# Where a transformer kernel forms its softmax totals and small weight sums: a change of places

## The chip, the cores and the metric

The kernel runs on one core of a Trainium2 chip. The core has a matrix engine (TensorE, written PE; its weight loads PEld), a vector engine (DVE), an activation engine (ACT), a general engine (GpSimd, written POOL) and SyncE (SP), whose queue (SPq) here only issues DMAs. The metric is the device time of one execution in microseconds. Three executions before the change took 2140.83, 2141.53 and 2144.35 us; the median is 2141.53.

## What is computed

The program runs two transformer layers over 16 sequences ("jobs" b = 0 to 15) of 256 tokens with 256 features, all in float32. Each layer has self attention, cross attention to a context and a feed-forward part:

```
x = attn(adaln(x), adaln(x)) @ wo + bo + x          # self, 16 heads of 64 in layer 0
x = attn(adaln(x), ln(context)) @ wo + bo + x       # cross
x = gelu(adaln(x) @ w1 + b1) @ w2 + b2 + x          # feed-forward
# layer 1 is the same with 16 heads of 16 and other modulations
```

The attention is softmax(q k^T / sqrt(d)) v, with rotary positions in layer 0. The softmax is taken without subtracting a maximum. Its denominators ("totals") are formed beside the products and multiplied into the attention's result before the output product.

## The kernel before

**Phases, jobs, steps.** Six phases follow each other: layer 0 self, layer 0 cross, layer 0 feed-forward, and the same three of layer 1. In each phase the jobs run b = 0 to 15; an attention job has two steps (s = 0, 1), a feed-forward job four. One list of steps is walked in order, and each engine's instructions stand in the order in which this walk writes them (a manual schedule). So an engine never passes over an instruction that waits, and the DMAs of SP are issued in the order written.

**One attention step of layer 0** (two groups of four heads, u = 2s and 2s + 1) does, for the current job, the rest of softmax and attention, and at the same time the preparation of the next step ("then"):

- The scores of the step were multiplied at the end of the step before (`scores`, `stage_s`, L768, on PE; L781, the exponentials, on ACT).
- `stage_t` (L787), `stage_turn` (L793) and `stage_reduce` (L800), all on DVE, add the exponentials over the two halves of the keys, transpose in blocks of 32 and sum. After four of each, job["rows"] is complete.
- `layer0_sums` (PE L839, ACT L849) multiplies the exponentials with the values; the result is job["raw"], four parts.
- For the next step, queries and keys are multiplied (`keys`, `query_part`, by Strassen's seven products once b is large enough: `queries_by_seven`, from b = 3 in self and from b = 4 in cross attention; `stage_rotary` with eight products before that). `rotate` and `stage_rotary` multiply by cosine and sine on DVE (L629, L636, L725) and form sums on POOL (L643, L733). The next scores need all of these sums.

**Totals.** `sum_up(job, at)` multiplies the rows with a small matrix on PE (`form_total`, "fold,rows"), takes the reciprocal on DVE (L813), sends it to DRAM by SP (L816) and fetches it back spread over the partitions (L819, which waits for the first DMA to land). `scale(job, *which)` multiplies parts 0 to 3 with it on POOL (L828). `fold_inner` then forms sums of the parts on POOL (L1121) for the output product, which `finish_folded` does in the next step in seven products, numbered 1 to 7, on PE; its additions to x follow on DVE (L1137 to L1148). `finish` (L1168) is the same with the plain product.

Where a job's total is formed depends on the step that follows it. From cross 4 on, `finish_folded(late, ..., total=job)` forms the current job's total at the end of its second step, so that the scaling in the next step ("early") finds it ready. Before that, and in self attention, the total of the previous job ("late") is formed in the first step of the next job, by sum_up(late, ...), and used in that same step.

**Weights' sums.** Strassen's products need sums of weights. `fold_query_weights` (POOL, L558 to L561) forms four of them for each half of the query weights; in cross attention the second half follows at the end of step s = 1 of b = 3, and query_part needs it from the next step on. `fold_output_weights` (DVE, L1031 to L1034) forms four for the feed-forward's second weight: in layer 0 in job 1's third step, in layer 1 in job 2's first, just after `pair_hidden` (L990, L1010, L1011, L1017, L1018 on DVE). `output_products(done, ...)` then does products 1 and 2 of the job two before in a second step, the others (4, 5, 6, 7, 3) in its fourth.

**The border.** `leaving` is true for b = 15 of a layer 0 attention phase. Its first step also loads the first half of the next phase's weights ("first") on SP, at the top of the step and so ahead of the step's totals. In cross attention, the job before it (14) gets its output product by finish(late, 7) in the second step of job 15, since no attention of layer 0 follows.

**Start.** `idle_products(n)` is n products of the identity with itself, into a bank that nothing reads. One call of 2 stands before `prepare_input(jobs[0])`.

## Time and profile before

| | |
|---|---|
| median of three runs | 2141.53 us |
| profiled execution | 2143.74 us |
| its span, first to last instruction | 2141.9 us |
| granted PE clock, mean over the span | 0.998 |
| ACT busy, DVE busy, POOL busy | 931.5, 1697.6, 1375.6 us |
| scores' products of a step in layer 0 (L768, x128) | 3.64 us |
| one scaling on POOL (L828), median | 1.28 us |
| one sum of parts on POOL (L1121), two tensors | 1.62 us mean |

The page has one row for each engine (busy time, share of the span, instructions). The chain of waits follows the last instruction back, at each point to what released it. The list of waits gives, for each pair of waiter and releaser, the sum, the number and the longest. The timeline gives the start and the length of instructions, equal neighbours merged with their number, and in brackets the idle time of the engine before it with what ended it. A PE product here is recorded as several matmul instructions that run side by side, so that the spacing of their starts, not their length, says how fast PE goes.

Where layer 0's self attention ends, the steps of PE stand so: self 14/1 from 603.04, self 15/0 from 623.09, self 15/1 from 642.21, cross 0/0 from 663.90 us (each after its scores).

### The profile page before, as it was taken

The numbers are of one execution on the slowest core, as the hardware profiler recorded it, in microseconds if no ns is written. First come the engines' busy times: TensorE is split into PE (matmuls) and PEld (weight loads), VectorE is DVE, ScalarE is ACT, GpSimd is POOL, SyncE is SP. The second block draws the span as 40 slices with busy tenths as digits, with TensorE's granted clock in tenths as the row PEclk, the third lists the DMA queues.
The fourth block names the chain that finished last, engine by engine and source line by source line (L and its number), as shares of the span: only waits on it lengthen the run. The fifth ranks groups of instructions, "written<-read, shape, count | busy, mean of one in ns | idle before, by whom it ended". The sixth has DMA issues, their size and how long they took to land.

```text
span 2141.9 us, 115148 instructions
## 1 busy us (share of the span) xinstructions
PE 2125.1 (99%) x52400; PEld 1472.1 (69%) x52400; DVE 1697.6 (79%) x3108; ACT 931.5 (43%) x1527; POOL 1375.6 (64%) x1498
## 2 busy tenths in 40 slices
PE   9999999999999999999999999999999999999998
PEld 5666767767766667677676768886665565566887
DVE  5878888888888888999998867865777777777765
ACT  3334334334333333443443344433666666665442
POOL 4888778778768788787878756662322223235773
PEclk9999999999999999999999999999999999999999
DMA  6110110110132321212212033221212232223321
GB/s 197 28 41 24 27 40 23 29 38 23 36 102 71 80 56 36 68 36 54 50 48 53 23 77 92 56 50 22 63 40 43 49 99 63 58 48 85 73 64 39
DMA packets 307050, 118.00 MB, mean 55 GB/s; under 512 B 243364, under 2 KB 289784, under 8 KB 306424
## 3 DMA queue, kind: packets, MB, share of 16 engines
q1 hardware_dynamic: 305320, 108.71, 20.6%
q8 instruction: 412, 6.75, 1.4%
q10 hardware_dynamic: 1232, 1.84, 0.2%
q14 instruction: 86, 0.70, 0.1%
HBM read 77.14 MB, written 33.29 MB: 52 GB/s over the span
## 4 chain that ended last, share of the span: by engine, by line
PE 85%; POOL 3%; DVE 3%; issue 1%; DMA 1%; SPq 0%; ACT 0%; DVEq 0%; POOLq 0%; ACTq 0%
PE banks L84 54%; PE banks L768 15%; PE banks L839 9%; PE banks L858 5%; PE banks L704 1%; PE banks L503 1%; POOL raw L828 1%; POOL folded L1121 1%; POOL qk L733 0%; DMA spread<-sums_seen 0%; DMA sums_seen<-inv 0%; DVE x L1075 0%; DVE m L629 0%; POOL qk L643 0%; DVE xh L365 0%
## 5 line engine op out<-in xcount | busy, mean ns | idle before, releaser
L781 ACT ACTIVATE pr<-banks 128x1024 f32<-128x1024 f32 x576 | 487.3, 937 | 450.1 <-PE banks L768 413.8
L643 POOL TENSOR_TENSOR qk<-m,m 128x256 f32<-128x256 f32 x400 | 303.9, 788 | 78.8 <-DVE m L636 47.2
L839 PE MATMUL banks<-pr,v 128*32 128x256 f32 x4096 | 244.8, 379 | 0.0
L768 PE MATMUL banks<-qk 32*64 32x256 f32 x8192 | 242.0, 379 | 2.6 <-POOL qk L643 1.8
L787 DVE TENSOR_TENSOR both<-pr 128x1024 f32<-128x1024 f32 x128 | 182.8, 1428 | 63.2 <-ACT pr L781 59.8
L768 PEld LDWEIGHTS banks<-qk 32*64 32x64 f32 x8192 | 186.2, 132 | 62.4 <-POOL qk L643 21.1
L828 POOL TENSOR_TENSOR raw<-raw,spread 128x512 f32<-128x512 f32 x128 | 168.5, 1337 | 50.8 <-DMA spread<-sums_seen 40.3
L839 PEld LDWEIGHTS banks<-pr,v 128*32 128x32 f32 x4096 | 131.4, 110 | 85.0 <-issue 16.8
L453 POOL TENSOR_TENSOR x<-x,bo_b 128x256 f32<-128x256 f32 x96 | 73.2, 782 | 163.2 <-DVE xh L365 163.2
L900 POOL TENSOR_TENSOR oT<-oT,spread 128x256 f32<-128x256 f32 x64 | 45.8, 738 | 205.3 <-DVE spread L899 205.3
L849 ACT COPY raw<-banks 128x512 f32<-128x512 f32 x128 | 75.0, 587 | 197.6 <-PE banks L839 192.5
L793 DVE STREAM_TRANSPOSE squares<-both 128x1024 f32<-128x1024 f32 x128 | 158.1, 1235 | 2.2
L800 DVE TENSOR_REDUCE rows<-squares 128x32 f32<-128x1024 f32 x128 | 154.8, 1209 | 0.9
L629 DVE TENSOR_TENSOR m<-banks,rope 128x512 f32<-128x512 f32 x200 | 128.3, 683 | 21.7 <-PE banks L84 12.1
L1121 POOL TENSOR_TENSOR folded<-raw,raw 128x512 f32<-128x512 f32 x90 | 143.5, 1623 | 2.4
L858 PE MATMUL banks<-pr,wide_v 128*32 128x256 f32 x2048 | 134.3, 379 | 0.0
L768 PE MATMUL banks<-q,k 32*64 32x256 f32 x4096 | 127.9, 381 | 0.0
L636 DVE TENSOR_TENSOR m<-banks,rope 128x512 f32<-128x512 f32 x200 | 125.2, 676 | 1.7 <-POOL qk L643 0.8
L84 PE MATMUL banks<-hT,wk_sa 128*32 128x256 f32 x2048 | 126.2, 381 | 0.0
L1075 DVE TENSOR_TENSOR x<-banks,x 128x256 f32<-128x256 f32 (+2 forms) x150 | 79.6, 531 | 56.1 <-PE banks L84 49.8
L768 PEld LDWEIGHTS banks<-q,k 32*64 32x64 f32 x4096 | 87.5, 131 | 37.7 <-issue 13.6
L733 POOL TENSOR_TENSOR qk<-m,m 128x512 f32<-128x512 f32 x56 | 78.3, 1419 | 35.3 <-DVE m L725 32.4
(289 smaller groups left out, 4577.8 us busy)
## 6 DMA issues: line engine op xcount, KB each, us to landing
turned<-blocks SPq DMA_DIRECT2D x380, 64.0 KB
fetched<-turned SPq DMA_DIRECT2D x380, 64.0 KB
spread<-sums_seen SPq DMA_DIRECT2D x128, 128.0 KB
x<-in_x SPq DMA_DIRECT2D x16, 256.0 KB
fetched_c<-turned_c SPq DMA_DIRECT2D x64, 64.0 KB
cT<-in_ctx_turned SPq DMA_DIRECT2D x16, 256.0 KB
out<-x SPq DMA_DIRECT2D x15, 256.0 KB
ctx<-in_ctx SPq DMA_DIRECT2D x16, 192.0 KB
```

Of the source, the lines that this page charges most:

```text
L84: nc.tensor.matmul(out[cut], lhsT[:, cut], rhs, start=start, stop=stop, **more)
L629: nc.vector.tensor_tensor(view, bank(2 + e if job["cross"] else 2 * e).rearrange("p (t h n) -> p t h n", t=2, h=2), rope[:, i, :].rearrang ...
L643: nc.gpsimd.tensor_tensor(out, cos[i], sin[1 - i], (ALU.subtract, ALU.add)[i])
L768: nc.tensor.matmul(banks[64 * g : 64 * g + 64, at + h, t * N : (t + 1) * N], lhs, rhs, start=(half == 0 and (t == 0 or job["layer"] == 1)) ...
L781: nc.scalar.activation(pr[:, one], sc[:, one], AF.Exp, scale=0.125 if job["layer"] == 0 else 0.25)
L787: nc.vector.tensor_tensor(both, pr[:, :, 0, :], pr[:, :, 1, :], ALU.add)
L793: nc.vector.transpose(job["squares"].rearrange("p b k -> p (b k)"), job.pop("both").rearrange("p h n -> p (h n)"))
L800: nc.vector.tensor_reduce(job["rows"][:, u, :], job.pop("squares"), AX.X, ALU.add)
L828: nc.gpsimd.tensor_tensor(part, part, spread[:, u : u + 1, :].to_broadcast([P, 2, N]), ALU.mult)
L839: nc.tensor.matmul(o[32 * h : 32 * h + 32, half, :], v[:, t, col : col + 32], pr[:, h, t, :], start=(t == 0), stop=(t == NT - 1),)
L858: nc.tensor.matmul(o[32 * h : 32 * h + 32], v[:, t, 4 * c + h, 32 * e : 32 * e + 32], pr[:, h, t, :], start=(t == 0), stop=(t == NT - 1),)
L1121: eng.tensor_tensor(folded[m], *sums[m])
```

## The change

All of it is in where instructions are written; none of the operations changes.

- Every step that is followed by a step of cross attention now passes total=job to finish_folded, so totals are formed at the second step's end for self 15 and cross 0 to 3 as well. `early` is computed for all branches, and in the branch without seven products the scaling is cut in two: parts 0 and 1 after the first rotary pair, 2 and 3 where all four were.
- In self 15/0, sum_up(late) goes up to just behind the first keys, into bank 3; scale(late, 0, 1) goes between rotate(1, 1) and rotate(0, 0), and 2 and 3 stay at the end.
- In cross 15/0 (`leaving`), parts 1, 2 and 3 are scaled together, and the output product of cross 14 is done here, ahead of the scores; finish(late, 7) in 15/1 is gone.
- fold_query_weights for the second half goes from the end of cross 3/1 to its beginning.
- fold_output_weights in layer 1 goes from job 2's first step to its second, behind output_products(done, 1, 2); the weights that are no sums (1 and 2) are set without it.
- The call of idle_products before the first input has 1 in place of 2.

```diff
@@ fold_output_weights, output_products
+        ph.setdefault("output_w", {1: b[0][0], 2: b[1][0]})
...
-        ph["output_w"] = {1: b[0][0], 2: b[1][0], 3: b[1][1], 4: t4, 5: t1, 6: t2, 7: t3}
+        ph["output_w"].update({3: b[1][1], 4: t4, 5: t1, 6: t2, 7: t3})
...
+        weights = job["phase"]["w"]["wo"]
+        job["phase"].setdefault("output_w", {1: weights[:, 0:4, 0:P], 2: weights[:, 4:8, 0:P]})
@@ before the loop
-    idle_products(2)
+    idle_products(1)
@@ feed-forward, s == 0
-            if b == 2 and s == 0:
-                if layer0:
-                    add()
-                else:
-                    fold_output_weights(job["phase"], nc.vector)
+            if b == 2 and s == 0 and layer0:
+                add()
@@ feed-forward, s == 1
                     output_products(done, 1, 2)
+                if b == 2 and not layer0:
+                    fold_output_weights(job["phase"], nc.vector)
@@ attention of layer 0, ahead of the branches
+            if weights_after == 1 and job["cross"]:
+                fold_query_weights(job["phase"], weights_after, nc.gpsimd)
+                weights_after = None
+            early = s == 0 and late is not None and "spread" in late
@@ cross, seven products
                 rotate(then, 1, 1)
                 if early:
-                    scale(late, 1)
+                    scale(late, *((1, 2, 3) if leaving else (1,)))
...
+                if s == 0 and leaving:
+                    add_late = finish(late, 7, later=True)
                 rotate(then, 0, 0)
                 query_part(then, 6)
                 rotate(then, 1, 0)
+                if s == 0 and leaving:
+                    add_late()
+                elif s == 0:
+                    scale(late, 2, 3)
                 if s == 0:
-                    scale(late, *((2, 3) if early else range(4)))
                     stage_turn(job, 1)
@@ self, seven products
                 keys(then, 0, 0)
-                if seven:
+                if s == 0:
                     sum_up(late, 3)
...
-                elif s == 0:
-                    sum_up(late, 6)
...
                     rotate(then, 1, 1)
+                    if s == 0:
+                        scale(late, 0, 1)
                     layer0_sums(job, 2 * s + 1, 5)
...
                     stage_turn(job, 2 * s + 1)
                     if s == 0:
-                        scale(late)
+                        scale(late, 2, 3)
@@ without seven products
                 rotary(then, 0, 1)
...
-                if late is not None and s == 0:
+                if early:
+                    scale(late, 0, 1)
+                elif late is not None and s == 0:
                     sum_up(late, 6)
@@ end of the step
                 if then and then[0]["cross"]:
-                    finish_folded(late, (4, 5), total=job if queries_by_seven(then) else None)
+                    finish_folded(late, (4, 5), total=job)
...
-                else:
-                    finish(late, 7)
             if late is not None and s == 0:
                 if not queries_by_seven(then):
-                    scale(late)
+                    scale(late, *((2, 3) if early else range(4)))
```

## The prediction

> **What bounds the kernel now.** The page's first part comes first. TensorE (PE) is busy in 99% of the span, and the chain of waits gives it 85%, so only time in which PE waits can be won or lost. The list of waits and the timeline then show where PE really stops: a few places, all at borders between phases. A step is called here by phase, job and step: "self 15/0" is the first step of the sixteenth job of layer 0's self attention.
>
> ```profile
> PE 2125.1 (99%) x52400; PEld 1472.1 (69%) x52400; DVE 1697.6 (79%) x3108; ACT 931.5 (43%) x1527; POOL 1375.6 (64%) x1498
> ...
> POOL raw L828 <- DMA spread<-sums_seen: 40.3, 18, 4.6
> ```
>
> The first line is the page's, the second one of the waits: 40.3 us in which the scaling on GpSimd (POOL) sat at the head of its queue until the spread sums had landed. Today hardly anything that PE needs soon is queued behind it.
>
> **Self 15/0: the scaling is put ahead of the rotary sums.** This is the timeline of that step (start, length, engine).
>
> ```profile
> 627.71 0.34 DVE L813 RECIPROCAL inv<-banks 128x32 f32<-128x32 f32 x1
> ...
> 628.75 0.56 SPq L283 DMA_DIRECT2D wk_ca<-in_ca_wkv  x1
> 629.40 1.40 SPq L284 DMA_DIRECT2D wq_ca<-in_ca_wq  x1
> 630.86 0.46 SPq L436 DMA_DIRECT2D ctx<-in_ctx  x1
> 631.44 0.39 SPq L816 DMA_DIRECT2D sums_seen<-inv  x1
> 633.09 2.81 POOL L643 TENSOR_TENSOR qk<-m,m 128x256 f32<-128x256 f32 x4 [2.68 <-DVE m L636]
> ...
> 636.11 1.42 POOL L643 TENSOR_TENSOR qk<-m,m 128x256 f32<-128x256 f32 x2 [0.20 <-DVE m L629]
> 636.28 1.94 SPq L819 DMA_DIRECT2D spread<-sums_seen  x4
> ...
> 638.57 3.71 PE L768 MATMUL banks<-qk 32*64 32x256 f32 x128
> ...
> 641.19 5.98 POOL L828 TENSOR_TENSOR raw<-raw,spread 128x512 f32<-128x512 f32 x4 [3.65 <-DMA spread<-sums_seen]
> ```
>
> The reader is to see that the sums land at 641.19, 2.6 us after PE has begun the next scores at 638.57. The change forms the total some 2 us earlier (just behind the first keys, 623.1). But the DMA of the reciprocals (L816) is not late for want of them: the reciprocal ended at 628.05, and SP was issuing without a break from 622.48 on (8 transposing DMAs, then two weight loads of 512 KB each and a context load, all ahead of L816 in the program, before and after). So L816 stays at 631.44 and the landing at 641.19. What moves is the scaling of the first two parts: it goes ahead of the last four rotary sums (L643, rotations 0/0 and 1/0), which the scores need. POOL reaches it at 634.5 (two of the four L643 at 633.09 are done), waits to 641.19, scales twice (2.53, from the pair at 595.65 in self 14/0), then forms the pair of L643 for the first scores (1.42): 645.15. PE can do 0.43 of the scores with the first of the two, so its new stall is 645.15 - 0.43 - 638.57 = **6.2 us**. The second pair comes at 646.6 and PE needs it 1.8 us after the first: no more.
>
> [...] L816 was issued at 631.44, and the spread, which waits for it, at 636.28, 4.4 us after SP had become free; one megabyte of weights is ahead in the same queue. In self 14/0, with no weights ahead, the same two issues are 588.53 and 590.75[...]. I take 641.19; the ends are 2.8 and 6.8.
>
> A stall of that length also costs clock. The table by windows, around PE's largest stall of today (cross 15/0; the columns are length, busy time of PE, PEld, DVE, ACT, POOL, then the granted clock and the DMAs):
>
> ```profile
> 1244.20:1247.60 3.40, 1.35 (x30) 0.80 (x38) 3.30 (x6) 0.00 (x0) 2.20 (x4) 1.00 0.64 207
> 1247.64:1251.05 3.41, 3.41 (x77) 2.60 (x69) 3.12 (x7) 1.08 (x2) 3.31 (x5) 0.50 0.09 27
> ```
>
> With PE busy 1.35 of 3.40 us, the next 3.41 us run at half clock, and after a full busy window the clock is back. Half clock lasts to the end of the first mostly busy window after the stall, so, with the phase unknown, 1.3 to 3.0 us are lost; I take **2.1**.
>
> Against this stands what a later PE no longer waits for at the border: in self 15/1 PE stands 0.83 and 0.34 for L1121 (its inner sums, which are late because the scaling came at 641.19) and 0.63 and 0.1 for the additions behind it. PE comes some 8 us later, POOL 2 (its folds end near 653.9 instead of 652.0), so all **1.9** go. Part: 6.2 + 2.1 - 1.9 = **+6.4**.
>
> **Totals early in self 15/1 and cross 0 to 3.** PE wins nothing directly: in cross 0 to 2 it has no stall today. New is that a total is formed in the second step, between products 7 and 6, and that PE waits there if the row sums (L800) are late. In cross 0/1, 1/1 and 2/1 they end at 696.03, 735.81 and 772.96; PE gets there near 697.8, 736.2 and 775.0: no wait, at worst 0.3 in the second. The first two scalings now go between the rotary pairs of the next step: in cross 1/0 POOL's second pair then ends at 718.6 instead of 717.5, and PE needs it at 719.3. SP now waits for the sums before the transposing DMAs of the step's end, as it does from cross 4 on. Cost 0; without that cover 0.5 to 1.
>
> **Query weights' sums at the start of cross 3/1.** Four POOL instructions, 1.70 + 0.73 + 1.71 + 0.74 = 4.9 us from the rows at 819.94 to 825.06. Today they lie behind the step and PE waits for two of them in the next: 0.96 + 0.47 = 1.4. Moved, they stand in POOL's queue ahead of this step's rotary sums, and POOL is late there already:
>
> ```profile
> 806.68 1.43 POOL L643 TENSOR_TENSOR qk<-m,m 128x256 f32<-128x256 f32 x2
> ...
> 812.03 1.29 DVE L629 TENSOR_TENSOR m<-banks,rope 128x512 f32<-128x512 f32 x2 [1.13 <-POOL qk L643]
> 813.24 1.21 DVE L800 TENSOR_REDUCE rows<-squares 128x32 f32<-128x1024 f32 x1
> ...
> 814.50 0.22 PE L84 MATMUL banks<-fold,rows 128*32 128x32 f32 x1 [0.99 <-DVE rows L800]
> ```
>
> Each line waits for the one before: POOL's L643 frees DVE's buffers, DVE's L629 holds up the row sum L800, and PE's total waits for that, 1.2 us today. POOL works from 792.6 to 814.8 without a break. New: two of the four scalings (2.5) move into cross 3/0, where POOL had only 1.5 idle, so they push 1.1; less 2.5, plus 4.9, makes it 1.1 - 2.5 + 4.9 = **3.5** later, and PE's total with it (near 818). PE's stall there becomes 4.7, 4.35 of it in one piece (the seventh product waits first for its own operand). Against it, the 1.4 in cross 4/0 go. Clock: the Trainium skill, "TensorE: Matmul & The Clock Gate", Part 1 ("The HAM clock gate"), lets the clock fall after at least one idle window of some 3.4 us. The 4.35 us hold a whole one in (4.35 - 3.41)/3.41 = 28% of phases, so nothing would be the likely cost. But in the first window row above PE was busy for 1.35, and the clock fell: some 2.5 us idle are enough, and 4.35 leave that in one window in three of four phases. I take the row: 0.77 x 2.1 = 1.6; ends 0 and 3.0. Part: 3.5 - 1.4 + 1.6 = **+3.7**. If POOL had the time free, it would be -1.4 to -2.6.
>
> **The last output product a step sooner (cross 15).** 128 PE instructions, 6.9 us by the 7.0 of the row at 1255.91, go from 15/1 into 15/0's stall, where PE waits 2.0 + 0.6 and then loses 1.7 at half clock. The third scaling ends near 1246.9, the product near 1251.3, the scores near 1255: 4.1 ahead of today. But what ends last is another chain. Row sums of job 15 need DVE for some 8 us behind the scores' exponentials (three kinds, two of each, 1.2 each, starting at about 1255.5): they end near 1263.5, against 1261.1 today, and PE, which now reaches the total at 1260.7, waits 3 us there; today the product covered this time and the total ran at 1264.33. Then the sums go through SP behind the transposing DMAs, as today, and land:
>
> ```profile
> 1275.15 5.01 POOL L828 TENSOR_TENSOR raw<-raw,spread 128x512 f32<-128x512 f32 x4 [4.58 <-DMA spread<-sums_seen]
> ```
>
> PE's product of job 15 follows these four scalings until 1280.2. Half clock after the new wait (one phase in three) would be taken from PE's 0.9 of waiting there. So 4.1 won becomes **-0.2**; ends -4.3 and +1.5.
>
> **Output weights' sums in layer 1's feed-forward 2.** Four DVE instructions, 0.69 each:
>
> ```profile
> 1959.33 1.07 PE L84 MATMUL banks<-inner,w_b 128*32 128x256 f32 x16 [1.38 <-DVE sums L1010]
> ```
>
> This wait (1.56 by the matmuls' spacing) goes. Behind L1011 of the second step the four end near 1960.3, and product 4 of the same job needs the last of them; PE would be there at 1959.5. New wait 0.85. Part **-0.7**; ends -1.6 and +0.5.
>
> **One idle product fewer.** Two PE instructions at half clock, 0.85 us at 9.6 to 11.4; PE's work then starts that much sooner, 0.43 in full-clock work. At 39.69 PE comes just as hT of job 1 is ready (it waited 7.6 for its DMA, behind SP's 13 loads of x up to 27.78), so the gain ends there: **0**; ends -0.4 and +1.7 (the clock rising a window later).
>
> **Sum.** 6.4 + 0 + 3.7 - 0.2 - 0.7 + 0 = **+9.2 us** on the profiled span of 2141.9 (the execution took 2143.74, 1.8 around it, which stay). On the median of 2141.53 that is **2150.7**.
>
> **Rivals.**
> - The sums land in time in self 15/0 (not slower). Each us by which they land after 635.0 (638.57 + 0.43 - 3.95) costs PE one; at or before it the step costs nothing and only the 1.9 are won: -1.9 + 3.7 - 0.9 = +0.9, 2142.4. For it: the total is formed 2 us sooner. Against it: SP's unbroken row of issues. 0.08.
> - The query sums do no harm (POOL makes up the 3.5): 6.4 - 1.4 - 0.9 = +4.1, 2145.6. For it: the scaling leaves POOL's queue there. Against: the unbroken POOL. 0.1.
> - All stalls are filled, -1.9 - 2.6 - 4.3 - 1.6: near 2131. It needs both of the above and a DVE that is sooner done in cross 15. 0.08.
> - Each new stall draws long half clock and 15/1's total another: +14, 2155.5. 0.1.
> - The forecast: 0.64, 2147 to 2155.
>
> About 0.2%, 4.3 us, is what a measurement can tell from no change. Faster is the third rival, 0.09 with small shares of others; same the first and half of the second, 0.13; slower the rest, 0.78. The range 2144 to 2158 leaves out the first and third rival and a little above.
>
> **What would show it.** Right: a PE wait of 5 to 7 us before L768 near 639, released by POOL L643, with POOL L828 waiting for the spread just ahead; half clock after it; no waits for L1121 at the border; the total in cross 3/1 waiting over 4 us for L800; that of cross 15 waiting 2 to 3; product 4 in layer 1's feed-forward waiting for DVE's fourth output-weight sum. Wrong: L816 issued before the weight loads, or POOL idle ahead of cross 3/1.

## The result and the profile after

| | before | after |
|---|---|---|
| median, four runs each | 2141.77 us | 2154.70 us |
| profiled execution | 2143.74 us | 2154.66 us |
| its span | 2141.9 us | 2152.8 us |

The change makes the kernel slower: the ratio is 1.0059, with a 95% interval of 1.0041 to 1.0076. The forecast was 2150.7 us, in a range of 2144 to 2158. By the medians the loss is 12.9 us; the profiled execution of before was 2.0 us above its median, so the two profiles differ by 10.9.

Where these 10.9 us come from can be read off the starts of the scores' products (L768 in the timeline), which both kernels do in the same order:

| PE begins | before | after | later by | gained since the row above |
|---|---|---|---|---|
| scores of self 15/0 | 619.25 | 619.17 | -0.08 | -0.1 |
| scores of self 15/1 | 638.57 | 645.14 | +6.57 | +6.7 |
| scores of cross 0/1 | 679.07 | 686.25 | +7.18 | +0.6 |
| scores of cross 4/1 | 835.38 | 842.66 | +7.28 | +0.1 |
| last scores ahead of cross 15 | 1231.04 | 1239.03 | +8.00 | +0.7 |
| first scores of layer 1 | 1469.75 | 1477.22 | +7.47 | -0.5 |
| last scores of layer 1 | 1930.31 | 1937.41 | +7.11 | -0.4 |
| end of the span | 2141.9 | 2152.8 | +10.96 | +3.9 |

So two places make the loss: the border behind self attention (7.3) and layer 1's feed-forward (3.9). The page's first part, which answers to the one shown of before, does not tell this: PE is busy in 99% of either span.

```profile
PE 2128.1 (99%) x52398; PEld 1472.1 (68%) x52398; DVE 1697.2 (79%) x3108; ACT 931.1 (43%) x1527; POOL 1370.9 (64%) x1498
```

The list of waits does, a little: the scaling's waits for its spread are fewer than before (15 for 18), but one is far longer (7.3 us for 4.6).

```profile
POOL raw L828 <- DMA spread<-sums_seen: 43.5, 15, 7.3
```

**Self 15/0.** The timeline of after, in the form in which that of before was shown:

```profile
625.33 0.34 DVE L813 RECIPROCAL inv<-banks 128x32 f32<-128x32 f32 x1
...
629.76 1.10 SPq L284 DMA_DIRECT2D wq_ca<-in_ca_wq  x1
...
631.49 0.39 SPq L816 DMA_DIRECT2D sums_seen<-inv  x1
...
637.38 1.93 SPq L819 DMA_DIRECT2D spread<-sums_seen  x4
...
641.92 2.48 POOL L828 TENSOR_TENSOR raw<-raw,spread 128x512 f32<-128x512 f32 x2 [7.33 <-DMA spread<-sums_seen]
...
644.36 2.77 POOL L643 TENSOR_TENSOR qk<-m,m 128x256 f32<-128x256 f32 x4
645.14 6.44 PE L768 MATMUL banks<-qk 32*64 32x256 f32 x128 [6.42 <-POOL qk L643]
```

The reciprocal ends 2.4 us sooner than before (625.67 against 628.05), but L816 leaves SP at the same time as before (631.49 against 631.44). POOL stands for 7.33 us before the scaling, the rotary sums L643 stand behind it, and PE behind them. The scores then take 6.44 us instead of 3.71: half clock.

**Cross 3/1.** Again the timeline. The four query sums (two of the rows are shown) and the chain from them to PE's total:

```profile
812.33 0.73 POOL L558 TENSOR_TENSOR ms_of_query_weights_True<-wq_ca 128x256 f32<-128x256 f32 x1
...
814.77 0.74 POOL L561 TENSOR_TENSOR ms_of_query_weights_True<-wq_ca,ms_of_query_weights_True 128x256 f32<-128x256 f32 x1
...
820.79 1.29 DVE L629 TENSOR_TENSOR m<-banks,rope 128x512 f32<-128x512 f32 x2 [2.23 <-POOL qk L643]
821.99 1.21 DVE L800 TENSOR_REDUCE rows<-squares 128x32 f32<-128x1024 f32 x1
823.26 0.22 PE L84 MATMUL banks<-fold,rows 128*32 128x32 f32 x1 [2.78 <-DVE rows L800]
```

The chain is the one of before, with 2.78 in place of 0.99. No sum takes 1.7 us here.

**Cross 15.** The product of job 14 now fills 15/0; the total waits for the row sum, and the last scaling for its spread:

```profile
1251.96 7.43 PE L84 MATMUL banks<-wo_ca,raw 128*32 128x256 f32 x128
1259.32 3.71 PE L768 MATMUL banks<-qk 32*64 32x256 f32 x128
...
1271.38 0.22 PE L84 MATMUL banks<-fold,rows 128*32 128x32 f32 x1 [2.28 <-DVE rows L800]
...
1282.87 4.99 POOL L828 TENSOR_TENSOR raw<-raw,spread 128x512 f32<-128x512 f32 x4 [4.87 <-DMA spread<-sums_seen]
```

**Layer 1, feed-forward 2.** DVE's four output-weight sums (L1032 to L1035 here), with what POOL does beside them:

```profile
1963.74 1.29 POOL L1045 TENSOR_TENSOR folded<-g 128x512 f32<-128x512 f32 x1
1963.87 0.69 DVE L1011 TENSOR_TENSOR g<-banks,sums 128x512 f32<-128x512 f32 x1
1964.48 1.10 DVE L1032 TENSOR_TENSOR output_w_L_xcond_b<-w_b 128x512 f32<-128x512 f32 x1
...
1965.61 1.65 DVE L1033 TENSOR_TENSOR output_w_L_xcond_b<-w_b,output_w_L_xcond_b 128x512 f32<-128x512 f32 x1
1966.68 1.71 POOL L1045 TENSOR_TENSOR folded<-g 128x512 f32<-128x512 f32 x1
1967.19 1.75 DVE L1034 TENSOR_TENSOR output_w_L_xcond_b<-w_b 128x512 f32<-128x512 f32 x1
1968.35 1.71 POOL L1045 TENSOR_TENSOR folded<-g,folded 128x512 f32<-128x512 f32 x1
1968.86 1.75 DVE L1035 TENSOR_TENSOR output_w_L_xcond_b<-w_b,output_w_L_xcond_b 128x512 f32<-128x512 f32 x1
...
1970.66 1.08 PE L84 MATMUL banks<-output_w_L_xcond_b,g 128*32 128x128 f32 x32 [4.10 <-DVE output_w_L_xcond_b L1035]
```

The four take 6.2 us in all instead of 2.8, and PE stands 4.1 us for the last, where it stood 1.4 for L1010 before.

### The profile page after: what moved, and what is told of

Read it like the earlier page. It is cut to its first block, busy times and chain, and to the rows that moved or that the text cites. A ratio compares the mean times of both kernels' runs of the same rounds, so it can differ in the third digit from the quotient of the medians.

```text
span 2152.8 us, 115151 instructions
## 1 busy us (share of the span) xinstructions
PE 2128.1 (99%) x52398; PEld 1472.1 (68%) x52398; DVE 1697.2 (79%) x3108; ACT 931.1 (43%) x1527; POOL 1370.9 (64%) x1498
## 4 chain that ended last, share of the span: by engine, by line
PE 85%; DVE 5%; POOL 2%; issue 1%; DMA 1%; ACT 0%; SPq 0%; DVEq 0%; POOLq 0%; ACTq 0%
PE banks L84 54%; PE banks L768 15%; PE banks L839 8%; PE banks L858 5%; PE banks L704 1%; PE banks L503 1%; DVE both L787 0%; DVE rows L800 0%; POOL raw L828 0%; DVE squares L793 0%; DVE m L636 0%; POOL folded L1124 0%; DVE m L629 0%; DVE x L1078 0%; DMA sums_seen<-inv 0%
## 5 line engine op out<-in xcount | busy, mean ns | idle before, releaser
L643 POOL TENSOR_TENSOR qk<-m,m 128x256 f32<-128x256 f32 x400 | 303.0, 785 | 75.8 <-DVE m L636 48.0
L768 PE MATMUL banks<-qk 32*64 32x256 f32 x8192 | 242.3, 381 | 6.7 <-POOL qk L643 6.4
L787 DVE TENSOR_TENSOR both<-pr 128x1024 f32<-128x1024 f32 x128 | 181.8, 1420 | 74.1 <-ACT pr L781 70.1
L768 PEld LDWEIGHTS banks<-qk 32*64 32x64 f32 x8192 | 186.1, 132 | 67.1 <-POOL qk L643 26.8
L828 POOL TENSOR_TENSOR raw<-raw,spread 128x512 f32<-128x512 f32 x128 | 166.3, 1319 | 61.8 <-DMA spread<-sums_seen 43.5
L453 POOL TENSOR_TENSOR x<-x,bo_b 128x256 f32<-128x256 f32 x96 | 73.1, 780 | 163.5 <-DVE xh L365 163.5
L800 DVE TENSOR_REDUCE rows<-squares 128x32 f32<-128x1024 f32 x128 | 154.7, 1209 | 0.9
L1124 POOL TENSOR_TENSOR folded<-raw,raw 128x512 f32<-128x512 f32 x90 | 140.5, 1589 | 2.3
L768 PE MATMUL banks<-q,k 32*64 32x256 f32 x4096 | 127.8, 381 | 0.0
L636 DVE TENSOR_TENSOR m<-banks,rope 128x512 f32<-128x512 f32 x200 | 125.2, 676 | 1.2 <-POOL qk L643 0.8
L768 PEld LDWEIGHTS banks<-q,k 32*64 32x64 f32 x4096 | 87.4, 131 | 37.6 <-issue 13.6
L357 POOL TENSOR_TENSOR rstd<-ve,neg_half 128x2 f32<-128x2 f32 x95 | 74.3, 782 | 50.0 <-DVE ve L355 45.6
```

The lines of the kernel that those rows point to most:

```text
L643: nc.gpsimd.tensor_tensor(out, cos[i], sin[1 - i], (ALU.subtract, ALU.add)[i])
L768: nc.tensor.matmul(banks[64 * g : 64 * g + 64, at + h, t * N : (t + 1) * N], lhs, rhs, start=(half == 0 and (t == 0 or job["layer"] == 1)) ...
L787: nc.vector.tensor_tensor(both, pr[:, :, 0, :], pr[:, :, 1, :], ALU.add)
L800: nc.vector.tensor_reduce(job["rows"][:, u, :], job.pop("squares"), AX.X, ALU.add)
L828: nc.gpsimd.tensor_tensor(part, part, spread[:, u : u + 1, :].to_broadcast([P, 2, N]), ALU.mult)
L1124: eng.tensor_tensor(folded[m], *sums[m])
```

## The experiments

Ten kernels were run in three groups. Each group ran on one chip, together with new runs of before (medians 2142.60, 2141.62 and 2141.55 us). The table gives, beside the times, what PE lost at four places, in us. It is worked out from the records of PE's instructions: the time by which each starts later than the one before it allows at full clock. So a stretch at half clock is contained in it; where there was one, its length stands in brackets (half of it is lost).

| kernel | median | ratio to before, 95% interval | self border (612 to 668) | cross 3/1, 4/0 | cross 15 | feed-forward 2, layer 1 |
|---|---|---|---|---|---|---|
| before | 2141.77 | 1 | 3.8 | 3.9 | 6.1 (3.4) | 1.8 |
| after | 2154.70 | 1.0059 [1.0041, 1.0076] | 10.7 (6.8) | 4.2 | 6.2 (3.4) | 6.0 (3.4) |
| a_scale_back | 2150.45 | 1.0042 [1.0026, 1.0059] | 4.4 | 4.0 | 6.0 (3.4) | 5.8 (3.4) |
| a_sums_first | 2151.60 | 1.0045 [1.0028, 1.0062] | 3.0 | 7.2 (6.8) | 6.6 (3.4) | 5.9 (3.4) |
| a_out_back | 2149.26 | 1.0034 [1.0022, 1.0047] | 8.7 (6.8) | 5.6 (3.4) | 5.4 | 1.8 |
| a_hidden_early | 2153.98 | 1.0056 [1.0039, 1.0073] | 10.4 (6.8) | 5.7 (3.4) | 5.9 | 3.8 |
| a_out_job1 | 2148.43 | 1.0029 [1.0018, 1.0041] | 10.3 (6.8) | 5.7 (3.4) | 6.4 | 0.0 |
| a_query_back | 2151.77 | 1.0049 [1.0034, 1.0063] | 9.3 (6.8) | 2.6 | 6.1 | 5.7 (3.4) |
| a_last_back | 2152.25 | 1.0053 [1.0038, 1.0069] | 8.6 (6.8) | 5.6 (3.4) | 4.8 | 5.7 (3.4) |
| b_best1 | 2137.24 | 0.9980 [0.9972, 0.9988] | 2.3 | 2.5 | 6.0 (3.4) | 0.4 |
| b_best2 | 2137.14 | 0.9978 [0.9969, 0.9987] | 2.3 | 1.5 | 5.7 | 0.0 |
| b_best3 | 2138.95 | 0.9988 [0.9981, 0.9994] | 2.8 | 1.5 | 8.5 (3.4) | 0.0 |

Each experiment is judged at its own place. The span also carries the half clock of the other places, which comes and goes (below), and the start: in after and the ten others the first scores began anywhere from 23.65 to 27.37 us (25.59 in before), though their code up to there is the same.

### a_scale_back: the scaling of self 15/0 in its old place

```diff
                     rotate(then, 1, 1)
-                    if s == 0:
-                        scale(late, 0, 1)
                     layer0_sums(job, 2 * s + 1, 5)
...
                     if s == 0:
-                        scale(late, 2, 3)
+                        scale(late)
```

> The changed kernel, but in self 15/0 all four scalings stand behind the rotary sums again; the total stays formed early. Theory (GpSimd's in-order queue: the scaling waits for the spread and holds up the rotary sums): the wait of PE before the next scores (6.4 us in the changed kernel) falls below 1 us, the half clock at 643.9 to 650.7 goes, the spread still lands near 641 to 642, and the waits for L1124 at the border (1.9 us) come back: the span falls by about 7.3 us from 2152.8 to some 2145.5. Rival (the early total or the other moves in that step cost the time): PE still stands more than 3 us in that step, and the span stays above 2150.

The spread landed at 641.33, as late as ever, and PE began the scores at 639.04 without a wait; no half clock followed. The border lost 4.4 instead of 10.7, so 6.3 us hang on the place of the scaling. One thing came otherwise. Of the waits for L1124 (L1121 in before) only 0.59 us came back, but PE stood 1.54 us for the row sum, at the total that the change forms in self 15/1:

```profile
659.75 0.22 PE L84 MATMUL banks<-fold,rows 128*32 128x32 f32 x1 [1.35 <-DVE rows L800]
```

So the early total is not free here; in after PE comes later and finds the row sum ready. The span fell by only 4.2, to 2148.7. This run was 1.6 us ahead at its first scores, but lost 1.8 more than after in self 14/0 (the spread landed at 595.84, no sooner than after's 595.76, with PE ready for it sooner), and 1.3 in layer 1 at 1746.85, both in code that is the same in the two. The theory holds at its place; the number for the span was missed.

### a_sums_first: the same scaling, its sums ahead of the weights in SP's queue

```diff
+        border_self = leaving and s == 0 and not job["cross"]
-        if leaving and s == 0:
+        if leaving and s == 0 and not border_self:
             load_phase(job["p"] + 1, "first")
...
+                if not border_self:
-                load_ctx(job_ahead)
+                    load_ctx(job_ahead)
...
                     sum_up(late, 3)
+                if border_self:
+                    load_phase(job["p"] + 1, "first")
+                    load_ctx(third)
```

> The changed kernel, but in self 15/0 SP issues the two weight loads and the context load behind the sums' DMAs instead of ahead of them; the scaling stays in its new place. Theory (the sums land late because of what stands ahead of them in SP's queue): L816 is issued near 629 instead of 631.5, the spread lands at 634 to 637 instead of 641.9, PE's wait before the scores is 0 to 1.5 us instead of 6.4, no half clock follows, and the span falls by 6 to 9 us to 2144 to 2147. Rival (the sums' way through memory takes 10 us whatever is ahead of it): landing at 639 or later, PE waits over 3.5 us, the span is 2149 or more. The loads themselves may come late: that would show as a wait of PE for wk_ca behind the scores of 15/1.

The timeline of this kernel in the same step:

```profile
629.91 0.55 SPq L816 DMA_DIRECT2D sums_seen<-inv  x1
...
632.87 1.76 SPq L819 DMA_DIRECT2D spread<-sums_seen  x4
...
637.64 2.51 POOL L828 TENSOR_TENSOR raw<-raw,spread 128x512 f32<-128x512 f32 x2 [1.64 <-DMA spread<-sums_seen]
...
640.88 3.97 PE L768 MATMUL banks<-qk 32*64 32x256 f32 x128 [0.76 <-POOL qk L643]
```

L816 goes 1.6 us sooner, and the way from its issue to the landing shrinks from 10.4 us (631.49 to 641.92) to 7.7. All of the 2.7 lies ahead of L819, which waits until L816 has landed: it follows 3.0 us behind L816 instead of 5.9. Both parts of the delay therefore come from the three loads ahead (two of weights, one of the context): 1.6 us from their place in SP's row of issues, the rest from the transfers themselves. Whether the bytes or the number of transfers counts there was not tested. PE's wait falls from 6.4 to 0.76 and the border loses 3.0, less than before the change. The span fell by only 3.2, since PE lost 3.0 more in cross 3/1, where the same wait as in after (3.05 us) was this time followed by 6.8 us at half clock.

### a_out_back: layer 1's output-weight sums in their old place

```diff
-            if b == 2 and s == 0 and layer0:
-                add()
+            if b == 2 and s == 0:
+                if layer0:
+                    add()
+                else:
+                    fold_output_weights(job["phase"], nc.vector)
...
-                if b == 2 and not layer0:
-                    fold_output_weights(job["phase"], nc.vector)
```

> The changed kernel, but layer 1's output-weight sums stand in their old place (first step of feed-forward job 2). Theory (these sums in their new place cost 3.7 us net): the four take 0.69 each again, PE waits 1.4 to 1.6 us for L1010 in that job and not for L1035, the half clock at 1971.7 goes, and the span falls by 3.7 to 4.4 us to about 2149. Rival (something else in layer 1 costs it): less than 1.5 us.

PE waits 1.56 us for L1010 again and nowhere for L1035; the place loses 1.8 instead of 6.0. The span fell by 5.4 to 2147.5, of which 4.2 are won here. The new place of these four instructions costs about 4 us.

### a_hidden_early: POOL kept idle beside them

```diff
+            ahead = b == 2 and not layer0
+            if s == 0 and ahead:
+                fold_hidden(done, nc.gpsimd, 5, 6, 7, 3)
             if s == 1:
-                if done is not None:
+                if done is not None and not ahead:
                     fold_hidden(done, nc.gpsimd, 5, 6, 7, 3)
```

> The changed kernel, but in layer 1's feed-forward job 2 GpSimd forms the four sums of job 0's hidden values one step earlier, so that it is idle while DVE forms the four output-weight sums in their new place. Theory (the two engines side by side slow each other): DVE's four take 0.7 us each instead of 1.1 to 1.75, PE waits 0.7 to 1.2 us for the last of them instead of 4.1, no half clock follows, and the span falls by about 4.4 us to 2148 to 2149. Rival (the sums are late by their place in DVE's queue alone, and long for another reason): they still take 1.1 to 1.75, PE waits about 4 us, the span stays within 1 us of 2152.8.

Only half of this came true, and the half that failed tells most. POOL was not idle: the addition of the output bias (L453) had slid into the free place. The timeline:

```profile
1967.53 1.02 DVE L1032 TENSOR_TENSOR output_w_L_xcond_b<-w_b 128x512 f32<-128x512 f32 x1
...
1967.96 2.31 POOL L453 TENSOR_TENSOR x<-x,bo_b 128x256 f32<-128x256 f32 x2
...
1968.58 1.10 DVE L1033 TENSOR_TENSOR output_w_L_xcond_b<-w_b,output_w_L_xcond_b 128x512 f32<-128x512 f32 x1
...
1969.61 1.21 DVE L1034 TENSOR_TENSOR output_w_L_xcond_b<-w_b 128x512 f32<-128x512 f32 x1
...
1970.74 0.68 DVE L1035 TENSOR_TENSOR output_w_L_xcond_b<-w_b,output_w_L_xcond_b 128x512 f32<-128x512 f32 x1
```

Three of the same four instructions overlap POOL's pair and take 1.0 to 1.2 us; the fourth begins after POOL has ended (1970.27) and takes 0.68. POOL's pair takes 2.31 instead of its usual 1.52. So the length follows POOL's work and not the instruction, its data or its place in DVE's queue. The wait for L1035 fell from 4.29 us to 2.78 and no half clock followed, but a wait of 1.0 for L1010 came up, behind DVE's normalization (L365), which now ran beside POOL's sums and took 2.72 us for its two instead of 0.73. The span hardly moved (2152.2).

### a_out_job1: the sums in job 1, where DVE was idle

```diff
             if s == 2:
                 if b == 1 and not layer0:
+                    fold_output_weights(job["phase"], nc.vector)
                     finish(jobs[j - 2], next_bank())
...
-                if b == 2 and not layer0:
-                    fold_output_weights(job["phase"], nc.vector)
```

> The changed kernel, but DVE forms layer 1's output-weight sums in feed-forward job 1, at the head of its third step, where the trace of before shows DVE and GpSimd both idle for 2.8 us. Theory (the sums cost what they cost because of the work beside and behind them in their place): the four take 0.69 each, PE waits neither for L1010 nor for L1035 in job 2, no half clock follows there, and the span falls by 5.5 to 6 us to about 2147 (1.6 of it below what the old place would give). Rival (the wait only moves): DVE's later output addition of layer 1 or the inner sums behind it hold PE up by 1 us or more in job 1, and less than 4 us are won.

```profile
1953.43 1.53 POOL L453 TENSOR_TENSOR x<-x,bo_b 128x256 f32<-128x256 f32 x2 [0.53 <-DVE xh L365]
...
1954.27 1.23 DVE L1032 TENSOR_TENSOR output_w_L_xcond_b<-w_b 128x512 f32<-128x512 f32 x1
1955.54 0.69 DVE L1033 TENSOR_TENSOR output_w_L_xcond_b<-w_b,output_w_L_xcond_b 128x512 f32<-128x512 f32 x1
```

The timeline of this kernel shows the same again: the first sum, beside POOL's L453, takes 1.23, the second, behind its end, 0.69 (as do the other two). The whole place loses nothing now, and the span fell by 5.8 us, as expected.

### a_query_back: the query sums at the end of cross 3/1 again

```diff
-            if weights_after == 1 and job["cross"]:
-                fold_query_weights(job["phase"], weights_after, nc.gpsimd)
-                weights_after = None
```

> The changed kernel, but the second half's query-weight sums stand at the end of cross 3/1 again; the early totals and scalings stay. Theory (GpSimd's queue sets the total's wait in cross 3/1: sums in it add, scalings out of it take away): the wait for L800 in 3/1 falls from 2.97 us to 0.5 or less (1.18 in before), the 0.96 and 0.47 in 4/0 come back, no half clock at either place, span down by 1.0 to 1.8 us, or by 3 to 5 more where the version compared has half clock behind that wait. Rival (DVE's own chain sets the wait): at least 1.2 us stay in 3/1, and the span does not fall.

The wait in 3/1 is gone altogether (2.97 in after, 1.18 in before), and the waits of 0.96 and 0.47 in 4/0 are back. So POOL's queue does set this wait: the two scalings that the change moves out of 3/1 are worth at least the 1.2, the four sums that it moves in cost at least the 3.0. The place loses 2.6 instead of 4.2, which is 1.6 less than in after and 1.3 less than in before. The sums took 1.69, 0.73, 1.72 and 0.73 us here, and 0.73 to 0.74 each in after. The timeline shows why two of them are long:

```profile
824.24 1.40 DVE L787 TENSOR_TENSOR both<-pr 128x1024 f32<-128x1024 f32 x1
824.54 1.69 POOL L558 TENSOR_TENSOR ms_of_query_weights_True<-wq_ca 128x256 f32<-128x256 f32 x1
```

L558 begins while DVE adds two tensors, and ends at 826.23, 0.59 behind DVE's end at 825.64: it did nearly nothing before. L560 does the same with DVE's next addition.

### a_last_back: the product of job 14 in cross 15/1 again

```diff
-                    scale(late, *((1, 2, 3) if leaving else (1,)))
+                    scale(late, 1)
...
-                if s == 0 and leaving:
-                    add_late = finish(late, 7, later=True)
...
+                else:
+                    finish(late, 7)
```

> The changed kernel, but the output product of cross job 14 stands in cross 15/1 again, and the second pair of scalings of 15/0 behind the rotary sums. Theory (the product fills a wait of 2.6 us in 15/0 and uncovers one of nearly the same size in 15/1, where DVE's chain of row sums ends at its own time): in 15/0 PE waits 2.0 and 0.6 us for L643 and L629 again, in 15/1 the 0.28 and 2.47 for L800 go, the start of layer 1 moves by less than 1 us against the changed kernel apart from the 1.7 that a stretch of half clock is worth. Rival (the move wins what it fills): layer 1 starts 2 us or more later than in the changed kernel, with as much half clock.

The waits of 2.02 and 0.58 in 15/0 are back, those of 0.28 and 2.47 for the row sum are gone. Layer 1 began 1474.55, against 1477.22, but PE was already 1.6 us ahead when it came to cross 15; the place itself lost 4.8 against 6.2.

The half clock of after does not account for this 1.4, though 3.4 us at half clock cost 1.7. Five other versions that contain the move had no half clock here, and the table shows that they lost hardly less: 5.4, 5.9, 6.4, 6.1 and 5.7 us, against 6.0 to 6.6 in the four with it. The last output product of the phase waits for the scaling (L828) anyway, and PE, when it comes sooner, stands longer. First a_hidden_early (no half clock), then after:

```profile
1283.81 1.07 PE L84 MATMUL banks<-wo_ca,raw 128*32 128x256 f32 x16 [0.23 <-POOL raw L828]
...
1287.51 4.52 PE L84 MATMUL banks<-wo_ca,raw 128*32 128x256 f32 x80 [0.17 <-POOL raw L828]
```

```profile
1285.19 7.25 PE L84 MATMUL banks<-wo_ca,raw 128*32 128x256 f32 x128
```

The two begin cross 15 within 0.2 us of each other. PE reaches the product 1.4 us sooner in the first, but starts on what follows it only 0.4 sooner (1291.85 against 1292.26). In the old place the clock does count: before lost 6.1 with half clock, a_last_back 4.8 without. So the move wins nothing: it is even where half clock comes in both places, and costs 0.6 to 1.6 us against the one profile of the old place without it. The medians of a_last_back and after (2152.25 and 2154.70, in different groups) cannot settle more.

### b_best1, b_best2, b_best3: what was learnt, put together

b_best1 joins the edits of a_sums_first, a_scale_back, a_out_job1 and a_query_back. b_best2 adds this (the second half's sum that needs no other is formed with the first half's, a job earlier), and b_best3 on top of it the next:

```diff
@@ b_best2: fold_query_weights
-        eng.tensor_tensor(s3, top[0], low[0], ALU.subtract)
+        if s == 0 or not ph["cross"]:
+            eng.tensor_tensor(s3, top[0], low[0], ALU.subtract)
+        if s == 0 and ph["cross"]:
+            other = ph["w"]["wq1"]
+            eng.tensor_tensor(ph["query_sums"][4], other[:, 0, N : 2 * N], other[:, 0, 0:N], ALU.subtract)
@@ b_best3: end of the step
+            put_off = leaving and job["cross"]
             if s == 0:
-                prepare_moments(third)
+                if not put_off:
+                    prepare_moments(third)
...
             else:
+                if put_off:
+                    prepare_moments(third)
                 prepare_norm(third)
```

> Four parts of what was learnt together: in self 15/0 the sums' DMAs ahead of the weight loads and the scaling in its old place, the query-weight sums in their old place, layer 1's output-weight sums in job 1; the last output product, the early totals and the single idle product as in the changed kernel. Theory: no wait over 0.3 us at the self border (1.9 in before), none for L1010 or L1035 in layer 1 (1.6), 3/1 below 0.5 (1.2), cross 15 as in the changed kernel (-0.5): span 2136 to 2138, ratio to before near 0.9975. Rival (each wait removed is given back a step later): ratio 0.999 or above.

> The version before, with one of the second half's four query-weight sums formed a job earlier, behind the first half's (end of cross 2/1), so that three are left at the end of 3/1. Theory: the waits for them in 4/0 (0.96 + 0.47) fall by 0.7 to 1.4 us, all else as in the version before: some 1 us less than it. Rival (those waits are set by the last sums' slow run beside DVE): no difference.

("The version before" is meant as the version just ahead, b_best1.)

> The version b_best2, and the moments of the job three ahead (two of L351, then L353 and L355, some 1.1 us of DVE between cross 15's second and third row sums) put behind the last row sum of 15/1. Theory (DVE's unbroken chain sets the last total in cross 15): the wait for L800 falls from 2.47 to about 1.3 us, too little for half clock, and the span falls by 1.1 us against b_best2 where that had none, to about 2135; ratio to before near 0.997. Rival (the chain waits for the scores' exponentials, or the put-off normalization holds up feed-forward job 2): the wait stays above 2 us, or PE waits a us or more for hT in layer 0's feed-forward.

b_best1 does what was expected at its places: no wait over 0.5 us is left at the self border, cross 3/1 has none, and the ratio is 0.9980. Its profiled execution was one of its longer ones (2141.04), with a wait of 1.77 in self 14/0, where the spread landed at 597.81 instead of before's 595.65. b_best2 takes the two waits in 4/0 away as well: 1.5 lost instead of 2.5. Between the medians of the two (0.1 us apart) that can't be told. The timeline of b_best2 in self 15/0, where L647 and L832 are the lines L643 and L828:

```profile
633.83 2.81 POOL L647 TENSOR_TENSOR qk<-m,m 128x256 f32<-128x256 f32 x4 [2.81 <-DVE m L640]
...
636.85 1.42 POOL L647 TENSOR_TENSOR qk<-m,m 128x256 f32<-128x256 f32 x2 [0.21 <-DVE m L633]
...
638.22 4.98 POOL L832 TENSOR_TENSOR raw<-raw,spread 128x512 f32<-128x512 f32 x4
...
639.30 3.71 PE L772 MATMUL banks<-qk 32*64 32x256 f32 x128
```

The scaling follows the rotary sums without a wait, 3 us sooner than before the change, and the border's waits for the sums of parts (1.9 in before) are gone.

b_best3 was a miss, in a way worth seeing. DVE's queue at the end of cross 15/1, and POOL's scaling:

```profile
1257.65 1.22 DVE L804 TENSOR_REDUCE rows<-squares 128x32 f32<-128x1024 f32 x1
1258.79 0.74 DVE L351 BATCH_NORM_STATS2 bn<-x 128x6 f32<-128x256 f32 x2
...
1262.12 0.32 DVE L817 RECIPROCAL inv<-banks 128x32 f32<-128x32 f32 x1
...
1273.09 4.94 POOL L832 TENSOR_TENSOR raw<-raw,spread 128x512 f32<-128x512 f32 x4 [5.55 <-DMA spread<-sums_seen]
```

The wait for the row sum fell by 0.3 only (2.47 to 2.19), because DVE now waited 0.79 for the scores' exponentials. And the moments, put behind the row sums, stood ahead of the reciprocal: L817 ran at 1262.12 instead of 1260.80, the spread landed 2 us later, and PE stood 3.4 us for it. b_best2 keeps the lowest ratio, 0.9978, which b_best1 shares within the noise; the interval of b_best3 just overlaps theirs. None of the three has job 14's product in its old place, so whether that would be better still is open.

## Why the prediction was right in sum, and where it was not

| step of the prediction | forecast | after, in the profile | the versions that contain it |
|---|---|---|---|
| self 15/0 | +6.4 | +7.3 | +4.8 to +6.9 (six) |
| totals early in self 15/1 and cross 0 to 3 | 0 | no wait | no wait, but 1.5 in a_scale_back (self 15/1) |
| query sums at the start of cross 3/1 | +3.7 | +0.1 | +0.1 to +3.3 (seven) |
| last output product a step sooner | -0.2 | -0.5 | -0.7 to +0.5 (nine, b_best3 apart) |
| output-weight sums in layer 1 | -0.7 | +3.9 | +3.8 to +4.2 (five) |
| one idle product fewer | 0 | -0.1 | not told apart from the start's own -1.9 to +1.8 |
| sum | +9.2 | +11.0 | |

(The last column is from the table of losses, less before's. The +0.7 between cross 4 and cross 15 and the -0.4 after belong to no step.)

**Self 15/0: right, by its own mechanism.** The stall was 6.6 us for a forecast 6.2, with the spread at 641.92 for 641.19. The half clock lasted 6.8 us in place of the one stretch behind the 2.1, since its first window had PE busy for only 2.18 us; from the scores' start on it cost 2.8. The border's own 1.9 went, as forecast. a_scale_back shows that POOL's order makes the wait, a_sums_first that SP's order makes the spread late. So the landing read from the row of before was right. With the loads behind, L819 followed L816 by 3.0 us instead of 5.9.

**Early totals: right in after, not free.** Beside the cost of 0 the prediction allowed 0.5 to 1. It looked for late row sums in cross 0 to 2, not in self 15/1, where PE waits 1.5 us once it comes without the new stall (a_scale_back).

**Query sums: the mechanism right, two terms too large.** The 3.5 by which PE's total was to come later (1.1 - 2.5 + 4.9) was really 2.97 - 1.18 = 1.8. The term that was mis-sized is 1.70 + 0.73 + 1.71 + 0.74: it was taken from a place where DVE added two tensors beside, and in the new place the four take 3.0 (1.1 - 2.5 + 3.0 is 1.6). The 1.4 in 4/0 went as said. The expected 1.6 for the clock did not come in this profile; in the seven versions with this wait it came in five. That is close to the three of four that the prediction took, but for a wait of 4.35, so the agreement is luck. The row behind it was also misread: PE busy 1.35 of 3.40 leaves 2.05 idle, not 2.5.

**Output-weight sums: wrong, with the wrong sign.** The step that failed is "Four DVE instructions, 0.69 each" behind L1011, "New wait 0.85". The order of the work was right, and so was the instruction that PE would wait for. But 0.69 is the price with POOL all but idle, as it was in the old place, and in the new place POOL forms job 0's hidden sums at the same time: 1.10 + 1.65 + 1.75 + 1.75 = 6.25. That makes a wait of 4.29 and a stretch of half clock. The rule was there to be read: the Trainium skill, "SBUF — State Buffer", section "Who interferes with whom", says that a DVE instruction with two SBUF inputs contends with a GpSimd instruction that reads SBUF, and calls the contention an exclusive lock. The trace agrees. With both engines in a row of such instructions, each takes 1.7, near the sum of 0.69 and 1.28 less some overlap; and L1011, which has one input in PSUM, took 0.69 right beside POOL's L1045 (the first two rows of that fence). The wrong length of the query sums, about half of that term's error, fits the same rule read from POOL's side: the price was taken beside DVE's L787, which adds two tensors of SBUF, and the new place is beside L636, which has one input in PSUM, and L800, which has one input. The two errors (3.6 and 4.6 us) had opposite signs and nearly cancelled: that the total is better than its parts is luck.

**Last product: right, by its own mechanism.** The new wait was 0.28 + 2.47 for a forecast 3, and the spread still ends the chain. The half clock behind the new wait is, as forecast, mostly taken from PE's waiting for the scaling. But the -0.5 of this pair of profiles says little: before had half clock here, and without it the old place lost less than the new one (a_last_back).

**The rivals.** That the query sums do no harm (2145.6) came true in its number at that place in this profile, but not in its reason: the wait of 2.97 is there, and other versions pay for it. That each new stall draws long half clock (2155.5) is nearest in time; in 15/0 it did, but the rest of that rival's sum was made by the output-weight sums, which no rival named. The sums landing in time, and all stalls filled, did not happen; a_sums_first and b_best2 show what they would have needed.

## What to carry to other kernels

- A duration belongs to its neighbours as much as to its instruction: before moving vector work, look at what the other of DVE and GpSimd does in the new place, and take the price from a row where both run (here 1.75, not 0.69).
- What an instruction waits for matters less than what is queued behind it. Forming a total earlier won nothing while SP's queue kept its DMA, and putting the scaling ahead of sums that PE needs cost 6 us. Small DMAs that something waits for go ahead of large loads.
- Judge an edit at its own place in the trace. The spans of these versions also carry a us or two of half clock at other places, by chance, and half clock ahead of a wait that would come anyway costs less than its length says (cross 15).

## What the runs showed beside it

**When the clock falls.** Equal waits had unequal price, and the windows show why. The clock changes on a grid of 3.41 us. Each pair below is a window of that grid and the next (columns: length, busy time of PE, PEld, DVE, ACT, POOL with counts, the granted clock, DMA share, GB/s). First after, then a_hidden_early, both around the wait of 2.47 us in cross 15/1; then a_last_back around the 2.0 + 0.6 in cross 15/0.

```profile
1268.55:1271.96 3.41, 1.13 (x20) 0.62 (x20) 3.34 (x6) 1.84 (x3) 2.93 (x4) 1.00 0.01 2
1271.96:1275.38 3.42, 3.42 (x40) 2.30 (x35) 2.57 (x11) 0.74 (x2) 2.66 (x5) 0.50 0.26 46
```

```profile
1266.86:1270.27 3.41, 2.10 (x38) 1.00 (x30) 3.34 (x4) 3.21 (x5) 3.41 (x3) 1.00 0.01 2
1270.27:1273.69 3.42, 2.45 (x49) 1.92 (x53) 3.39 (x11) 0.43 (x2) 2.92 (x4) 1.00 0.02 5
```

```profile
1248.77:1252.18 3.41, 1.81 (x52) 1.19 (x43) 2.22 (x5) 0.58 (x1) 2.52 (x4) 1.00 0.24 76
1252.18:1255.59 3.41, 2.91 (x93) 2.23 (x100) 3.38 (x4) 0.25 (x1) 3.09 (x5) 1.00 0.55 196
```

In after the wait falls into one window, PE is busy for 1.13 of it, and the next runs at half clock. In a_hidden_early the grid cuts the same wait in two, PE is busy for over 2 us in both, and nothing happens. a_last_back has the wait of before in cross 15/0, whose rows are in the prediction (busy 1.35, then half clock); cut in two, it leaves 1.81 and 2.91 and costs no clock. With the first and last 15 us of each span left out, the twelve profiles hold 22 windows at full clock with PE busy for 1.44 us or less, and every one was followed by half clock; of the 7388 others, with 1.53 or more, none was. The limit lies near 43% of a window. (Close to the ends it does not hold: in a_query_back a window from 7.04 with 2.07 us busy was followed by half clock, in after one from 2145.77 with 1.43 was not.) The way back has a limit too: the seven half-clock windows with PE busy for 2.68 us or less were followed by a second one, those with 2.83 or more by full clock. That is why some stretches last 6.8 us. Of nine profiles with the wait of 2.47, four had the stretch; of seven with that of 2.97 in cross 3/1, five. So a wait of 2.5 to 3 us costs its length and, about every second time, half clock: 1.7 more for one window, 3.0 for the two in a_sums_first, and less where a later wait takes it up.

**A wait that nothing shows.** In two of the twelve profiles (a_scale_back, a_hidden_early) PE stood 1.3 and 1.4 us within a step of layer 1 (at 1746.85 and 1752.97), for nothing that the profile names and in code that no version touches. What it was stays open.
